# Graph attention where sets of twelve rows meet only the nodes they need, their rows gathered by indirect DMAs

## The chip, the core and the metric

The kernel runs on one core of one Trainium2 chip. The metric is the device time of one execution in microseconds; the kernel before takes 2598.82 us (median of 3 runs, 2598.19 to 2600.02). Engines are named as in the profile: PE is TensorE, DVE VectorE, ACT ScalarE, POOL GpSimd, SP the engine that only issues DMAs.

## The reference

Two layers of graph attention over 8 graphs of 2048 nodes that share one adjacency matrix `adj`, and a layer norm. The first layer has 4 heads of 64 features, the second one head.

```python
def _gat_layer(h, mask, b):
    scores = jnp.einsum('...nd,...md->...nm', h, h)
    scores = jnp.where(mask, scores, NEG)
    attn = jax.nn.softmax(scores, axis=-1)
    return jnp.einsum('...nm,...md->...nd', attn, h) + b
mask = graph + jnp.eye(N, dtype=graph.dtype) > 0
h = jnp.einsum('bnc,hdc->bhnd', x, Wh)
out_h = _gat_layer(h, mask[None, None], bh[None, :, None, :])
cat = jnp.transpose(out_h, (0, 2, 1, 3)).reshape(B, N, H * D)
z = jax.nn.leaky_relu(cat, negative_slope=0.2)
h2 = jnp.einsum('bnk,dk->bnd', z, Wo)
out2 = _gat_layer(h2, mask[None], bo)
z2 = jax.nn.leaky_relu(out2, negative_slope=0.2)
out = (z2 - mu) * jax.lax.rsqrt(var + LN_EPS) * gamma + beta
x = _layernorm(x + out, axis=-1)
```

The entry of `adj` for nodes n and m is 1 with a probability of 0.0039 times a weight of n and a weight of m, and the weights fall with the node's number: the first nodes have many neighbours (177, 130, 110 ...), those from number 56 on seven on average.

## The kernel before

Both kernels are two programs behind each other. `fast_kernel` shifts scores by a constant instead of each row's maximum, and writes a flag when its sums leave the range in which this is safe. `gat_kernel` reads the flag, and `general_kernel`, which is exact for all inputs, runs only if it is set. In the execution profiled it does not run.

The fast program has 20 units: four pairs of graphs, each with four units of the first layer (one graph, two heads) and one of the second (two graphs). A unit has 4 chunks of 512 nodes and for each of them 16 steps over the other nodes, 128 at a time: 1280 steps in all. The loop over `steps` writes out, step after step: `scores` (L560: 4 matmuls of 64x64 weights and 512 columns on the four quarters of the PE array, into a PSUM tile `s`; L563 on DVE takes the mask off; L564 on ACT is the exponential), and three steps later (`LAG`) `values` (L573: 4 matmuls with the exponentials as moving operand, added up in `o`). The sums of the exponentials are formed by `add_up` on POOL (L604) and by accumulating DMAs that POOL issues (L593), and joined by `sums` (L639). Every node meets every node; the mask adds a large negative number where `adj` has no entry.

What follows a chunk (`join`, `leaky`, `invert`, `scale`, `project`, `norm`) is handed to later steps by `at`, a table from step to jobs. `load_adj` (L478) brings `adj` in 32 pieces of 512 KB, `mask_rows` (L483) turns them into numbers on ACT, `mask_turn` transposes them. `prepare` turns a unit's maps with small matmuls of 64x64 weights and 64 columns (L438).

Order is fixed by the code: the fast program is written under a manual schedule, so each engine runs its instructions as written, and a semaphore holds one back only until its operands and its buffer are there.

## Time and profile before

| What | Value |
|---|---|
| median of 3 runs | 2598.82 us |
| the profiled execution | 2602.55 us |
| its span on the core | 2600.8 us |
| its granted PE clock | 0.991 |
| PE records of matmuls | 26414, two for each f32 matmul |
| PE, DVE, ACT, POOL busy | 97, 70, 66, 78% |
| DMA | 144027 packets, 289.62 MB, 111 GB/s on average |
| HBM read and written | 42.40 MB and 4.46 MB |

In a row of a group stand the line, the engine, the operation, output and inputs with their shapes, the count; after the bar the busy time in us and the mean time of one in ns; after the second bar the time that the engine idled before such instructions, and what ended the waits. Groups of weight loads are named PEld; they run beside the matmuls. Several matmuls run at once on parts of the array, so the mean time of one is longer than the distance between two starts.

### The profile page before, as it was taken

The page shows a single profiled execution, that of the slowest core. Times are in us where ns is not written, and L with a number is a line of the kernel's source. Part 1 is how long each engine was busy: PE and PEld are TensorE (multiplying, and loading weights), DVE is VectorE, ACT ScalarE, POOL GpSimd, SP SyncE. Part 2 cuts the span into 40 slices and gives each one's busy share as a digit, 9 for nine tenths or more (in the row PEclk, how much of TensorE's full clock was granted, in tenths as well). Part 3 has the DMA queues.
Part 4 walks back from the last instruction along what each step waited for, and adds up shares of the span by engine and source line. Part 5 has one row for each costly group of instructions (what it writes and reads, how often), then busy time and mean ns, then how long its engine had stood idle before and what let it go on. Part 6 is the DMA issues. An engine that isn't in the chain of part 4 may idle for free.

```text
span 2600.8 us, 61515 instructions
## 1 busy us (share of the span) xinstructions
PE 2512.0 (97%) x26414; PEld 891.4 (34%) x26414; DVE 1812.2 (70%) x1755; ACT 1706.5 (66%) x1721; POOL 2037.0 (78%) x1265
## 2 busy tenths in 40 slices
PE   7999999999999999999999899999999999999996
PEld 3333333333333333333333233333333333333332
DVE  5876677677777577666777676766676777676775
ACT  5776666666666566666666566666666666666664
POOL 5788788788767888778867887887888788875776
PEclk9999999999999999999999999999999999999998
DMA  4326566556555556656655465655565566655553
GB/s 138 104 77 120 102 116 128 102 107 122 114 100 115 114 107 113 132 101 113 118 116 109 96 121 112 128 110 103 113 116 107 107 123 118 116 112 98 115 113 79
DMA packets 144027, 289.62 MB, mean 111 GB/s; under 512 B 50658, under 2 KB 75298, under 8 KB 143746
## 3 DMA queue, kind: packets, MB, share of 16 engines
q0 software_dynamic: 65552, 238.32, 49.2%
q1 hardware_dynamic: 62722, 46.76, 6.1%
q8 instruction: 208, 3.41, 0.5%
q10 hardware_dynamic: 15472, 0.53, 0.5%
q14 instruction: 73, 0.60, 0.1%
HBM read 42.40 MB, written 4.46 MB: 18 GB/s over the span
## 4 chain that ended last, share of the span: by engine, by line
PE 72%; DMA 9%; POOL 5%; ACT 4%; DVE 4%; issue 3%; ACTq 1%; SPq 0%; POOLq 0%; DVEq 0%
PE s L560 34%; PE o L573 31%; PE pz L639 4%; DMA e<-e 3%; DVE e L563 3%; DMA zt<-zsb 3%; POOL acc L604 2%; DMA z<-rd 1%; ACT e L564 1%; DMA rd<-rt 1%; PE pn L438 1%; POOL acc L607 1%; ACTq L652 1%; PE o L682 1%; ACT hT L524 1%
## 5 line engine op out<-in xcount | busy, mean ns | idle before, releaser
L563 DVE TENSOR_TENSOR e<-s,mask 128x1024 f32<-128x1024 f32 x1280 | 1560.9, 1222 | 661.2 <-PE s L560 634.9
L564 ACT ACTIVATE e<-e,shifts 128x1024 f32<-128x1024 f32 x1280 | 1467.3, 1148 | 799.9 <-DVE e L563 753.1
L573 PE MATMUL o<-e,hN 64*64 64x512 f32 x10240 | 1332.8, 591 | 2.9 <-ACT h2T L689 2.1
L604 POOL TENSOR_TENSOR acc<-acc,e 128x1024 f32<-128x1024 f32 x452 | 1158.5, 2563 | 86.0 <-ACT e L564 71.4
L560 PE MATMUL s<-hT 64*64 64x512 f32 x8192 | 1076.0, 596 | 28.4 <-DVE e L563 9.4
L573 PEld LDWEIGHTS o<-e,hN 64*64 64x64 f32 x10240 | 391.9, 133 | 714.4 <-issue 586.8
L560 PEld LDWEIGHTS s<-hT 64*64 64x64 f32 x8192 | 296.2, 133 | 596.5 <-issue 436.7
L593 POOL DMA_DIRECT2D e<-e x454 | 398.5, 968 | 99.6 <-ACT e L564 61.6
L560 PE MATMUL s<-h2T 64*64 64x512 f32 x2048 | 267.8, 593 | 0.3 <-DVE e L563 0.2
L601 POOL TENSOR_TENSOR acc<-e,e 128x1024 f32<-128x1024 f32 x80 | 190.6, 2383 | 28.8 <-ACT e L564 18.8
L607 POOL TENSOR_TENSOR acc<-acc,e 128x1024 f32<-128x1024 f32 x60 | 142.1, 2368 | 76.6 <-DMA e<-e 75.6
L560 PEld LDWEIGHTS s<-h2T 64*64 64x64 f32 x2048 | 75.0, 134 | 137.5 <-issue 114.5
L639 PE MATMUL pz<-e,ones 128*32 128x512 f32 x616 | 116.4, 601 | 1.2 <-DVE e L563 0.7
L639 PE MATMUL pz<-acc,ones 128*32 128x512 f32 x320 | 85.4, 613 | 20.2 <-POOL acc L607 20.1
L734 POOL TENSOR_TENSOR st<-st,mhalf 128x8 f32<-128x8 f32 x32 | 57.3, 1791 | 49.7 <-ACT st L733 49.7
L673 POOL TENSOR_TENSOR z<-u,z 128x512 f32<-128x512 f32 x32 | 40.9, 1277 | 57.5 <-DMA z<-rd 48.8
L642 ACT COPY zsb<-pz 128x512 f32<-128x512 f32 x80 | 45.9, 574 | 52.3 <-PE pz L639 51.2
L673 POOL TENSOR_TENSOR u<-u,z 128x512 f32<-128x512 f32 x32 | 40.9, 1277 | 47.3 <-DMA z<-rd 40.5
L744 POOL TENSOR_TENSOR y<-y,st 128x512 f32<-128x512 f32 x15 | 15.6, 1041 | 74.1 <-ACT st L743 69.4
L627 DVE TENSOR_TENSOR u<-o,o 128x512 f32<-128x512 f32 x80 | 55.2, 690 | 6.9 <-ACT o L622 3.5
L618 DVE TENSOR_TENSOR o<-o,oj 128x512 f32<-128x512 f32 x80 | 55.9, 699 | 4.6 <-ACT oj L614 3.1
L552 DVE TENSOR_TENSOR hN<-pn,bhb 128x1024 f32<-128x1024 f32 x32 | 39.2, 1225 | 27.1 <-PE pn L438 26.9
(82 smaller groups left out, 769.4 us busy)
## 6 DMA issues: line engine op xcount, KB each, us to landing
e<-e POOLq DMA_DIRECT2D x454, 512.0 KB, 5.6
adj<-in_adj_dram SPq DMA_DIRECT2D x32, 512.0 KB, 4.6
z<-rd SPq DMA_DIRECT2D x128, 128.0 KB, 3.4
x<-in_x_dram SPq DMA_DIRECT2D x16, 256.0 KB, 4.1
xr<-in_x_dram SPq DMA_DIRECT2D x32, 128.0 KB, 2.4
out_dram<-y SPq DMA_DIRECT2D x32, 128.0 KB, 5.5
zt<-zsb SPq DMA_DIRECT2D x160, 2.0 KB, 5.0
zt<-zsb ACTq DMA_DIRECT2D x160, 2.0 KB, 5.4
```

What stands on the lines that cost most here:

```text
L560: nc.tensor.matmul(ps[k * 64:(k + 1) * 64, j, :], self.hT[rows, m * P + k * 64:m * P + (k + 1) * 64], self.hT[rows, c * W:(c + 1) * W], st ...
L563: nc.vector.tensor_tensor(e, ps, mask[c][:, m, :].unsqueeze(1).to_broadcast([P, 2, W]), OP.subtract)
L564: nc.scalar.activation(e, e, AF.Exp, bias=shifts[:, 1:2] if self.second else shifts[:, 0:1], scale=1.0)
L573: nc.tensor.matmul(self.O[c][j * D:(j + 1) * D, r, :], self.hN[rows, m, j * D:(j + 1) * D], e[rows, j, :], start=(m == 0), stop=(m == NB - 1))
L593: nc.gpsimd.dma_start(out=self.first[k], in_=e, accum_op=OP.add)
L601: nc.gpsimd.tensor_tensor(acc, self.acc, e, OP.add)
L604: nc.gpsimd.tensor_tensor(self.acc, self.acc, e, OP.add)
L607: nc.gpsimd.tensor_tensor(self.acc, self.acc, self.first[k], OP.add)
L618: nc.vector.tensor_tensor(b, b, self.t, OP.add)
L639: nc.tensor.matmul(pz[q:q + 32, :W], ones, terms[s * half + k][:, j, :], start=(k == 0), stop=(k == half - 1), tile_position=(0, q))
L673: nc.gpsimd.tensor_tensor(dst, self.u[c], self.z[c], OP.mult)
L734: nc.gpsimd.tensor_tensor(st[:, 2, :], st[:, 1, :], mhalf, OP.pow)
```

## The change

The fast program is replaced; the exact one stays. The flag's program and the check remain in kind, with other conditions.

The first 56 nodes (`HUB`) are treated as before in kind: each meets all nodes, in 16 blocks of 128 (`hub_scores`, `hub_values`), for all 8 graphs. The other 1992 nodes form 166 sets of 12 (`SET`): set s has the nodes 56 + s, 56 + s + 166, and so on. A set needs the union of its twelve rows of `adj`. The kernel makes one number per set and node: bit k is set where row k needs the node, times 2048, plus the node's number (`make_keys`: matmuls with powers of two add twelve rows of `adj` up). DVE picks for each set the 128 largest of these (`pick`: eight classes of 256 nodes by number modulo 8, the 32 largest of each by `max` and `match_replace`, eight at a time, then the 128 largest of those 256). A transpose makes them columns: `index` holds the node of each of the 128 slots, and `mask` which of the twelve rows need it. `over` keeps the last kept number of each class and set; if one is still a needed node, the flag is set. Sets are sorted in two rounds, 84 and 82 sets; the first in the hub phase, the second inside layer 1.

`table1` in DRAM has a row of 8 x 65 numbers for each node (8 graphs, 64 features and a one). An indirect DMA on POOL (`gather`) brings the 128 rows of a set, 266 KB. The column of ones makes each sum of exponentials a 65th column of the values. Scores of the first layer are x'(W'W)x: `gram` holds W'W for each head, `columns` multiplies it to the set's own twelve nodes, `scores` multiplies that to the gathered rows, turned by 64x64 matmuls with the identity (`turn`). The values are sums of x, and `heads` applies W after that. Two sets are a group; 83 groups run through layer 1 in a loop of stages written out by hand. `second_maps` and `second_rows` write the second layer's maps to `table2`, from which layer 2 gathers, four sets at a time (42 units); `back` and `norm_sets` bring its results to rows of 120 nodes for the two norms, in parts spread over units by `spread`.

The core of the diff (all of the function's lines of before are removed; PSUM has two buffers for each of the tags `s` and `o`; NG is 83, NU 42, LOOK 4):

```diff
-    epool = ctx.enter_context(tc.tile_pool(name="epool", bufs=13))
...
-    steps = [(u, c, m) for u in units for c in range(NC) for m in range(NB)]
-    total = len(steps)
...
+    rowp = ctx.enter_context(tc.tile_pool(name="rowp", bufs=12))
+    def two(name, tag="s"):
+        return psum.tile([P, 2, 512], F32, tag=tag, name=name)
+    def turn(tp, j, rows):
+        v = tp.rearrange("c r (j q i) -> c r j q i", j=2, q=Q)
+        for q in range(Q):
+            for p in range(2):
+                for r in range(2):
+                    nc.tensor.matmul(v[half(p), r, j, q, :], rows[half(r), 2 * q + p, :D], ident[half(r), half(r)],
+                                     start=True, stop=True)
...
+    def load_adj(r, c, t):
+        s0, n = ROUNDS[r]
+        raw = early.tile([84, 2, 512], I32, tag="raw", name=f"raw{r}_{c}_{t}", bufs=3)
+        nc.sync.dma_start(out=raw[:n], in_=byset[s0:s0 + n, 2 * t:2 * t + 2, c * 512:(c + 1) * 512])
+        a = early.tile([84, 2, 512], BF16, tag="a", name=f"a{r}_{c}_{t}", bufs=7)
+        nc.gpsimd.tensor_scalar(a[:n], raw[:n], 1.0, 0.0, OP.min, OP.max)
...
+    def top(src, dst, last):
+        def job():
+            nc.vector.max(out=dst, in_=src)
+            if not last:
+                nc.vector.match_replace(out=src, in_to_replace=dst, in_values=src, imm_value=-1.0)
+        return job
...
+    def gather(table, s, layer):
+        t = rows[layer, s] = rows_tile(f"g{layer}_{s}")
+        nc.gpsimd.indirect_dma_start(out=t.rearrange("p b k -> p (b k)"), out_offset=None, in_=table,
+                                     in_offset=bass.IndirectOffsetOnAxis(ap=index[:, s:s + 1], axis=0))
...
+    def values(g):
+        op = two(f"o{g}", "o")
+        e = es[g % 2]
+        for j in range(2):
+            rw = rows.pop((1, 2 * g + j))
+            for q in range(Q):
+                for p in range(2):
+                    c0 = (p * 8 + q * 2 + j) * M
+                    nc.tensor.matmul(op[half(p), j, q * K1:(q + 1) * K1], e[:, c0:c0 + 64], rw[:, 2 * q + p, :],
+                                     start=True, stop=True)
+        osb = held["o", g] = work.tile([P, 2, Q, D], F32, tag="osb", name=f"osb{g}")
+        invert(op, rall[:, g, :].rearrange("p (s q) -> p s q", s=2), osb, P, Q)
...
+    for i in range(-2, NG + 5):
+        for g in ([i + LOOK] if i > -2 else range(0, LOOK - 1)):
+            if 0 <= g < NG:
+                for j in range(2):
+                    gather(table1, 2 * g + j, 1)
...
+        if 0 <= i < NG:
+            values(i)
+        if 0 <= i + 1 < NG:
+            scores(i + 1)
+        if 0 <= i + 2 < NG:
+            tp, t = turn_group(1, i + 2, "s")
+            nc.scalar.copy(t, tp)
+        if 0 <= i - 1 < NG:
+            heads(i - 1)
+        if 0 <= i < NG:
+            turn_values(i)
+        if i >= 0:
+            for _ in range(2):
+                if pieces:
+                    r, c, k = pieces.pop(0)
+                    load_adj(r, c, k)
+                    if k == SET // 2 - 1:
+                        make_keys(r, c)
...
+    for u in range(-2, NU + 10):
+        for v in ([u + 3] if u > -2 else range(1, 2)):
+            if 1 <= v < NU:
+                for s in sets[v]:
+                    gather(table2, s, 2)
...
+        if 0 <= u + 1 < NU:
+            scores2(two(f"s2_{u + 1}", "o"), sets[u + 1], es[(u + 1) % 2])
+        if 0 <= u + 2 < NU:
+            for g in sorted({s // 2 for s in sets[u + 2]}):
+                tp, t = turn_group(2, g, "s")
+                (nc.scalar.copy if g % 2 else nc.vector.tensor_copy)(t, tp)
+        if 0 <= u < NU:
+            values2(sets[u], es[u % 2])
```

How the order changes on the engines is shown at three places; a row has the line, the operation, output and inputs by name and number, the shape and how often it comes in a row. First PE in the middle of layer 1. Before, scores `s` and values `o` alternate:

```order
L560 MATMUL s_2_11_3178<-hT_0_184 64x512 x4
L573 MATMUL o_2_3038<-e_2_8_3130,hN_2004 64x512 x4
L560 MATMUL s_2_12_3191<-hT_0_184 64x512 x4
L573 MATMUL o_2_3038<-e_2_9_3143,hN_2004 64x512 x4
L560 MATMUL s_2_13_3204<-hT_0_184 64x512 x4
```

Now one turn of the loop has these rows (`hyr` holds the second layer's maps, the set's own columns and the second layer's rows; `o` the values, `s` the scores, `t` the turned rows `g`, `cat` the heads, `ot` the turned values):

```order
L792 MATMUL hyr_7629<-z_7452,woT 64x96 x4
L737 MATMUL hyr_7629<-xT,gram 64x96 x8
L798 MATMUL hyr_7629<-ident,own 48x128 x2
L767 MATMUL o_7651<-g_76_7029,e_152 64x65 x8
L767 MATMUL o_7651<-g_77_7031,e_152 64x65 x8
L749 MATMUL s_7671<-y_7494,xTg_39_7590 64x48 x32
L509 MATMUL t_40_7706<-ident,g_80_7327 64x64 x16
L509 MATMUL t_40_7706<-ident,g_81_7329 64x64 x16
L525 MATMUL cat_7741<-otb_7623,whT 64x96 x8
L779 MATMUL ot_7755<-ident,osb_7668 64x48 x16
```

Eight matmuls of 512 columns a step have become 118 of 48 to 128 columns a group; the whole fast program has 18062 matmuls for 13721. Second, DVE and ACT at the same place. DVE's turn of the loop, from the copy of the own columns `y` to the half of `leaky` that writes `z`:

```order
L739 COPY y_7643<-hyr_7629 128x384
L803 COPY rowt_156<-hyr_7629 48x2x64
L515 RECIPROCAL rall<-o_7651 128x8
L516 TENSOR_TENSOR osb_7668<-o_7651,rall 128x512
L752 TENSOR_TENSOR e_153<-s_7671,mask 128x768
L534 SCALAR_TENSOR_TENSOR z_7750<-cat_7741,bhp,z_7750 128x192 x2
```

ACT's turn beside it:

```order
L756 ACTIVATE e_152<-e_152,shifts 128x768
L865 COPY xTg_41_7888<-t_41_7855 128x1024
L533 ACTIVATE z_7899<-cat_7890,bhf 128x192 x2
L781 COPY otb_7921<-ot_7904 128x384
L794 COPY own<-hyr_7927 128x96
L803 COPY rowt_154<-hyr_7927 48x2x64
```

Where a step before had one pass of 1024 on each, a group has six passes on each, and `leaky` stands behind the mask on DVE and behind the copy of the turned rows on ACT. Third, POOL in layer 2. Before, POOL adds exponentials and issues accumulating DMAs:

```order
L593 DMA e_0_0_7837<-e_0_8_7986 128x1024
L593 DMA e_0_1_7853<-e_0_9_8000 128x1024
L604 TENSOR_TENSOR acc_0_7926<-acc_0_7926,e_0_10_8015 128x1024
L604 TENSOR_TENSOR acc_0_7926<-acc_0_7926,e_0_11_8031 128x1024
L734 TENSOR_TENSOR st_3_8057<-st_3_8057,mhalf 128x8
```

Now it has a unit's four gathers into `g`, and now and then a power for a norm:

```order
L721 DMA g_44_16762<-table_136,index 128x520
L721 DMA g_45_16764<-table_136,index 128x520
L721 DMA g_46_16766<-table_136,index 128x520
L721 DMA g_47_16768<-table_136,index 128x520
L973 TENSOR_TENSOR st_15988<-st_15988,mhalf 120x8
L973 TENSOR_TENSOR st_16383<-st_16383,mhalf 120x8
```

The sums on POOL and the accumulating DMAs are gone; 332 gathers have come, each held back in POOL's order until one of the 12 row buffers `g` is free.

More of the change, by code (lines that the diff above doesn't have):

```diff
@@ L39 @@
 FMAX = 3.4028234663852886e38
-BIG = 255.0
+HUB = 56
+SET = 12
 SHIFT1 = 78.0
@@ L459, in fast_kernel @@
[L459 to L468 removed]
+    table1 = dram.tile([N, ROW], F32, name="table1")
@@ new lines, in turn_values @@
+    def turn_values(g):
+        pt = two(f"ot{g}", "o")
+        osb = held.pop(("o", g))
+        for q in range(Q):
+            for j in range(2):
+                for p in range(2):
+                    r = slice(p * 64, p * 64 + M)
+                    nc.tensor.matmul(pt[half(j), p, q * M:(q + 1) * M], osb[r, j, q, :], ident[r, r], start=True, stop=True)
+        ot = held["ot", g] = work.tile([P, H, 2 * Q * SET], F32, tag="ot", name=f"otb{g}")
+        nc.scalar.copy(ot.rearrange("c h (p n) -> c h p n", p=2),
+                       pt[:, :, :Q * M].rearrange("c p (n h) -> c h p n", h=H))
@@ new lines, in hub_block, with hub_turn @@
+    def hub_block(w):
+        for j in range(2):
+            t = rows["h", 2 * w + j] = rows_tile(f"gh{2 * w + j}")
+            i = 2 * w + j
+            nc.sync.dma_start(out=t.rearrange("p b k -> p (b k)"), in_=table2[i * P:(i + 1) * P, :])
+    def hub_turn(w):
+        tp = two(f"th{w}")
+        for j in range(2):
+            turn(tp, j, rows["h", 2 * w + j])
+        t = held["T", "h", w] = work.tile([P, 2, 512], F32, tag="xTg", name=f"xTgh{w}", bufs=3)
+        nc.scalar.copy(t, tp)
@@ new lines, in fast_kernel @@
+    nc.vector.tensor_reduce(tot[:, 4:5], over.rearrange("p r k -> p (r k)"), AX.X, OP.max)
+    nc.vector.tensor_scalar(tot[:, 4:5], tot[:, 4:5], float(N), None, OP.is_lt)
+    nc.vector.tensor_reduce(tot[:, 5:6], tot[:, 0:5], AX.X, OP.min)
+    pf = two("pf")
+    nc.tensor.matmul(pf[0:1, 0, 0:1], tot[:, 5:6], ones, start=True, stop=True)
+    fl = late.tile([1, 1], I32, name="fl", bufs=1)
+    nc.vector.tensor_scalar(fl, pf[0:1, 0, 0:1], P - 0.5, None, OP.is_lt)
+    nc.sync.dma_start(out=flag, in_=fl)
```

932 lines of the change are left out of this document (536 added, 396 removed).

## The prediction

> **What bounds the kernel now.** I read the page from the top (span and busy shares), then the chain that ended last, then the two dearest groups.
>
> ```profile
> span 2600.8 us, 61515 instructions
> ...
> PE 2512.0 (97%) x26414; PEld 891.4 (34%) x26414; DVE 1812.2 (70%) x1755; ACT 1706.5 (66%) x1721; POOL 2037.0 (78%) x1265
> ...
> PE 72%; DMA 9%; POOL 5%; ACT 4%; DVE 4%; issue 3%; ACTq 1%; SPq 0%; POOLq 0%; DVEq 0%
> ...
> L573 PE MATMUL o<-e,hN 64*64 64x512 f32 x10240 | 1332.8, 591 | 2.9 <-ACT h2T L689 2.1 <-ACT e L564 0.7
> ```
>
> TensorE is busy 97% and idles 2.9 us before 10240 value records: it is the bound, and every score is computed, masked or not. The change takes most scores away, so what counts is what a small matmul costs. The timeline of TensorE has one burst of them between two of the large ones (start, length, group):
>
> ```profile
> 906.12 1.11 PE L438 MATMUL pn<-ident,hT 64*64 64x64 f32 x64
> 907.05 1.04 PE L560 MATMUL s<-hT 64*64 64x512 f32 x8
> 907.92 1.04 PE L573 MATMUL o<-e,hN 64*64 64x512 f32 x8
> ```
>
> Each f32 matmul leaves two records. Starts differ by 0.93 us for 64 records of 64 columns: **14.5 ns each**. Eight of 512 columns take 0.87 us, four quarters of the array running at once: 0.85 ns a column on one quarter, 0.21 on four, 0.42 on two.
>
> **Layer 1, one pair of sets (83 of them).** Records on TensorE, in the order of the change's listing of one turn of the loop: 8 of 96 columns on half the array (0.32 us), 16 such (0.64), 4 of 128 (0.21), 32 of 65 for the values (0.87), 64 of 48 for the scores (at 14.5 ns 0.93), 64 turns (0.93), 16 of 96 on a quarter (0.32), 32 of 48 (0.46). Sum 4.7 us. The other engines' durations:
>
> ```profile
> L563 DVE TENSOR_TENSOR e<-s,mask 128x1024 f32<-128x1024 f32 x1280 | 1560.9, 1222 | 661.2 <-PE s L560 634.9 <-POOL acc L604 10.7 <-issue 5.7
> L564 ACT ACTIVATE e<-e,shifts 128x1024 f32<-128x1024 f32 x1280 | 1467.3, 1148 | 799.9 <-DVE e L563 753.1 <-issue 37.2 <-ACT e L564 0.9
> ...
> L618 DVE TENSOR_TENSOR o<-o,oj 128x512 f32<-128x512 f32 x80 | 55.9, 699 | 4.6 <-ACT oj L614 3.1
> ...
> L614 ACT COPY oj<-o 128x512 f32<-128x512 f32 x80 | 45.6, 570 | 1.3 <-PE o L573 1.0
> ...
> L524 ACT COPY hT<-ph 128x1024 f32<-128x1024 f32 x32 | 31.8, 995 | 1.3 <-PE ph L522 1.2
> ...
> L660 DVE RECIPROCAL rt<-zall 128x8 f32<-128x8 f32 x80 | 16.3, 203 | 2.8
> ...
> L731 DVE TENSOR_REDUCE st<-sq 128x8 f32<-128x512 f32 x16 | 11.0, 686 | 11.8 <-ACT sq L718 11.8
> ...
> L507 DVE COPY whT<-pw 128x256 f32<-128x256 f32 x1 | 0.4, 425 | 7.7 <-PE pw L506 7.7
> ```
>
> Read between these rows by width, VectorE does 384 + 64 + reciprocal + 512 + 768 + 2x192 in 3.4 us, ScalarE 768 + 1024 + 2x192 + 384 + 96 + 64 in 3.6. No engine is full, so the period comes from a loop. The accumulator `o` has two buffers for three uses, and the values of pair i+1 take the buffer that the heads of pair i-1 leave when `leaky` has read it. Going round: values 0.87, reciprocal and product 0.20 + 0.70, mask 0.96 (queued behind them on VectorE), exp 0.87, copy of the turned rows 1.0 and two `leaky` passes 0.66 (in ScalarE's order behind the exp), VectorE's last half 0.35, seven hand-overs 0.4. **6.0 us a pair.** The hand-overs are an estimate from these rows of the timeline, where the exp begins 0.04 us after the mask ends; those to and from TensorE are taken a little longer:
>
> ```profile
> 900.36 1.22 DVE L563 TENSOR_TENSOR e<-s,mask 128x1024 f32<-128x1024 f32 x1 [0.49 <-PE s L560]
> ...
> 901.62 1.15 ACT L564 ACTIVATE e<-e,shifts 128x1024 f32<-128x1024 f32 x1 [0.57 <-DVE e L563]
> ```
>
> Pairs fall into three stretches. 57 run free: 342 us. In 14 the second sort shares VectorE: four jobs a pair, a max and a replace over 256 elements each, priced with the 256-wide row (0.425 each, so 3.4 us); with the two copies that stand behind them (0.56 + 0.28) the loop becomes 9.15 us, 128 us in all. In the first 12 pairs the second half of adj arrives.
>
> **Second-half adj: the number of engines.** 24 transfers of 82 rows x 2 x 2 KB = 336 KB, three in flight, with the pass over each on POOL ahead of later gathers and the keys in TensorE's queue: if they are late, all is late.
>
> ```profile
> q1 hardware_dynamic: 62722, 46.76, 6.1%
> ...
> adj<-in_adj_dram SPq DMA_DIRECT2D x32, 512.0 KB, 4.6
> z<-rd SPq DMA_DIRECT2D x128, 128.0 KB, 3.4
> x<-in_x_dram SPq DMA_DIRECT2D x16, 256.0 KB, 4.1
> xr<-in_x_dram SPq DMA_DIRECT2D x32, 128.0 KB, 2.4
> out_dram<-y SPq DMA_DIRECT2D x32, 128.0 KB, 5.5
> zt<-zsb SPq DMA_DIRECT2D x160, 2.0 KB, 5.0
> ...
> rd<-rt SPq DMA_DIRECT2D x64, 4.0 KB, 2.9
> ...
> flag<-fl SPq DMA_DIRECT2D x1, 0.0 KB
> ```
>
> The window of 14 to 20 us, with DMA share and GB/s last:
>
> ```profile
> 14.00:20.00 6.00, 5.18 (x56) 1.91 (x57) 1.94 (x2) 3.04 (x4) 1.62 (x4) 1.00 0.99 320
> ```
>
> A transfer's data packets are the contiguous runs of its tile. By the shapes in the code SP's 465 transfers hold 55296 of them beside the flag (adj 32x512, z 128x64, x 16x128, xr and out 32x128 each, zt 128x64 + 32x128, rd 64x128). 62722 (the first figure of the queue's row) less those is 7426 = 464x16 + 2: a transfer of 64 or 128 rows ends in 16 packets, one per DMA engine, and the one-row flag in one, beside its data. So the rows decide how many engines serve a transfer, and 82 = 2x41 rows go in equal shares to two engines and not to 16. The window (DMA share 0.99, 320 GB/s) gives 20.2 GB/s an engine. Ends: on 16 engines a transfer takes 1.0 us and is hidden; on two 8.3 us, 200 us for 24. I take **200 us**, since equal shares fit what the packets show. [...]
>
> **Gathers.** 332 on POOL, 266 KB each, an operation that the trace does not have.
>
> ```profile
> L604 POOL TENSOR_TENSOR acc<-acc,e 128x1024 f32<-128x1024 f32 x452 | 1158.5, 2563 | 86.0 <-ACT e L564 71.4
> L593 POOL DMA_DIRECT2D e<-e x454 | 398.5, 968 | 99.6 <-ACT e L564 61.6 <-DMA e<-e 34.7 <-issue 3.1
> ...
> L734 POOL TENSOR_TENSOR st<-st,mhalf 128x8 f32<-128x8 f32 x32 | 57.3, 1791 | 49.7 <-ACT st L733 49.7
> ...
> L468 POOL DMA_DIRECT2D bob<-in_L_gnn_bo_dram x2 | 1.1, 569 | 0.0
> ```
>
> From 0.57 (128 plain rows) to 2.56 (POOL's dearest pass); I take 0.97, the other transfer that POOL issues row by row. Landing: 4.1 us, as x, of equal size. In layer 1 that is 1.9 us of 6.0, issued four pairs ahead: hidden. **In layer 2 it is not.** Its 12 row buffers are three units of four sets; the gathers of unit u+3 wait, in POOL's queue, until `values2` of unit u has read its rows, and TensorE wants them in the next unit. From the end of `values2`: the first buffer was free 0.7 us earlier, the fourth gather starts 2.9 us after that (2.2), lands at 6.3, 64 turns to 7.2, `values2` (64 records) to 8.2. **8.2 us a unit, 42 units, 344 us.** Beside it TensorE has 256 records, 4.7 us or less; VectorE 384 + a 1024 copy 1.2 + the norms (14 passes of 0.69 and small ones, 10.5 us per 2.5 units) and waits, 6.7; POOL 3.9 + pow 1.4.
>
> **The rest.** The adj passes are ScalarE's now:
>
> ```profile
> L483 ACT ACTIVATE mrow<-adj,shifts 128x1024 bf16<-128x1024 int32 x32 | 36.3, 1134 | 0.0
> ```
>
> On POOL one may take 1.13 to 2.56 us; I take 2.0, nearer to the row of its own engine. Start and blocks 0 to 3: 24 such passes and 8 us before them, 56. Blocks 4 to 8, under the first sort: 87 steps of 0.425, masks 7, their own VectorE 12: 56. Seven blocks more: TensorE 3.7 (turns, 32 records of 224 columns, 32 of 65 on the whole array), with waits 4.6: 32. Hub ends: twice eleven dependent steps of 0.5, and 6 for the first groups: 17. Between the layers: five draining turns at 2, 7 for `table2` to land and be read, eight steps of layer 2's hubs at 3.3 (a 1024 copy, an 896 exp, the masks, hand-overs), 6 to fill: 49. The end: a norm's 10.5 on VectorE, `back` out and in at 2.9 each (as `rd`), its steps' hand-overs and powers 6, `out` 5.5, the flag 2: 30. These are estimates from the rows shown.
>
> Sum: 56 + 56 + 32 + 17 + 200 + 128 + 342 + 49 + 344 + 30 = 1254, and 1.75 outside the span (profiled 2602.55 against 2600.8): 1256. The median shown, 2598.82, is 0.14% under the profiled execution: **1254**.
>
> **Rivals.**
> 1. All 16 engines serve the 82-row transfers. Nothing in the trace has such a row number. Twelve pairs then cost 6.5 us with the keys' matmuls, 78 for 200: **1132**.
> 2. A gather costs POOL 2.5 us, for it must read 128 indices. Layer 1 still hides 5.0; in layer 2 the fourth starts at 6.8, 12.8 us a unit, +194: **1448**. Against it: 0.57 and 0.97 for the plain ones.
> [...]
> 4. Slower: a set needs over 128 slots or a class over 32, or a sum leaves its bounds; the flag is set and the exact program runs behind. Its values alone are 5120 matmuls of 256 columns on the whole array, two records each: 2.2 ms, so over **3450**. Counted on the reference's inputs, the fullest set needs 119 slots, the fullest class 26, and logs of the sums lie from -57.7 to 78.7 where -63 to 83 pass.
>
> **How the numbers follow.** Forecast 48%, rivals 24, 17, 8 and 3%. The range runs from rival 1 with the loop or the gather somewhat cheaper (0.57 a gather takes 50 us off) to rival 2 with 20 more: 1040 to 1470. 0.2% is about what a measurement can tell from no change; only rival 4 is not faster by more.
>
> **What would show it.** Second-half adj landing in 20 us or more, and TensorE waiting for POOL's `a` and the keys in the first 12 pairs (16 engines: under 6 us). Pairs 6.0 us apart, with `o` waiting for `leaky`. Units 8 us apart, with the turns of layer 2 waiting for DMA; if for POOL's queue and 12 us, the gather's price is wrong. Units under 7 us would mean that rows land sooner than 4 us. TensorE's records of 64 columns at 14 ns, or not.

## The result, and the profile after

The changed kernel takes **1776.5 us** (median of 4 runs, 1767.7 to 1788.1) beside 2599.4 us for the kernel before (4 runs, 2598.2 to 2601.9): ratio 0.684, 95% interval 0.680 to 0.688. The profiled execution took 1767.7 us, 512 us more than the 1255.8 us of the prediction's sum. The sign was right, the size was not. One remark is needed for later numbers: the experiments ran on four chips, and the unedited changed kernel takes 1771 to 1789 us on one of them and 1956 us on another, so each experiment is read against the run of the changed kernel that has the same time for a pair of sets.

The page of the changed kernel: span, busy shares, the granted clock in 40 slices, the chain of work that ended last, and four of its groups and issues (columns as before).

```profile
span 1765.9 us, 77071 instructions
...
PE 1205.0 (68%) x35983; PEld 1063.5 (60%) x35983; DVE 705.3 (40%) x1427; ACT 453.4 (26%) x818; POOL 449.3 (25%) x467
...
PEclk9669866666777887887877888887866665666665
...
PE 9%; issue 8%; DMA 6%; POOL 4%; DVE 3%; ACT 1%; SPq 1%; POOLq 0%; DVEq 0%; ACTq 0%
...
L721 POOL DMA_INDIRECT g<-table,index x332 | 323.3, 974 | 1040.3 <-PE o L767 595.2
L509 PE MATMUL t<-ident,g 64*64 64x64 f32 x10624 | 278.0, 268 | 62.5 <-DMA g<-table,index 50.1
...
L644 POOL TENSOR_SCALAR a<-raw 84x1024 bf16<-84x1024 int32 (+1 forms) x48 | 49.7, 1036 | 211.2 <-DMA raw<-in_adj_dram 211.0
...
g<-table,index POOLq DMA_INDIRECT x332, 4.2
```

No engine is full any more. TensorE went from 97% to 68%, with 9600 more records than before, and its clock, nearly full in the kernel before (0.991), is now between 0.6 and 0.9 of full in almost every slice (0.736 on average). A gather costs GpSimd 0.974 us and lands after 4.2 us, as priced (0.97, 4.1).

Three stretches of layer 1 and the units of layer 2 in windows (length; busy time and count for PE, PEld, DVE, ACT, POOL; granted clock, DMA share, GB/s):

```profile
200.00:400.00 200.00, 95.59 (x2585) 76.09 (x2577) 40.49 (x77) 36.47 (x73) 50.61 (x60) 0.69 0.23 71
400.00:575.00 175.00, 115.86 (x3268) 104.86 (x3272) 90.25 (x237) 43.89 (x92) 28.49 (x31) 0.74 0.20 54
575.00:1150.00 575.00, 411.02 (x12143) 366.97 (x12136) 182.36 (x361) 173.96 (x364) 96.33 (x102) 0.80 0.21 55
...
1300.00:1690.00 390.00, 306.03 (x11530) 281.98 (x11534) 203.37 (x334) 94.83 (x136) 189.48 (x170) 0.64 0.50 137
```

These counts give the pace: a pair has 236 records of matmuls, so the third row is 12143 / 236 = 51.5 pairs, 11.2 us each; a unit has 320, so the fourth is 36.0 units, 10.8 us each. The prediction had 6.0 and 8.2. By its terms:

| Stretch | predicted us | measured us |
|---|---|---|
| start to the first pair (56 + 56 + 32 + 17) | 161 | 192 |
| 12 pairs while the second half of adj arrives | 200 | 208 |
| 14 pairs with the second sort | 128 | 174 |
| 57 free pairs | 342 | 626 |
| between the layers | 49 | 72 |
| 42 units | 344 | 426 |
| end, from the last values | 30 | 68 |

One free pair in the timeline of the changed kernel (start, length, engine, group, and in brackets the idle time before it with what ended it):

```profile
800.10 0.25 ACT L794 COPY own<-hyr 128x96 f32<-128x96 f32 x1
...
800.41 1.52 PE L737 MATMUL hyr<-xT,gram 128*64 128x96 f32 x16 [1.85 <-ACT own L794]
802.04 0.56 DVE L739 COPY y<-hyr 128x384 f32<-128x384 f32 x1 [1.75 <-PE hyr L737]
...
802.66 0.67 PE L798 MATMUL hyr<-ident,own 128*48 128x128 f32 x4 [0.73 <-DVE y L739]
...
803.11 1.95 PE L767 MATMUL o<-g,e 128*64 128x65 f32 x32
...
804.99 2.08 PE L749 MATMUL s<-y,xTg 64*64 64x48 f32 x64
...
806.82 1.89 PE L509 MATMUL t<-ident,g 64*64 64x64 f32 x64
...
808.51 0.52 PE L525 MATMUL cat<-otb,whT 64*64 64x96 f32 x16
...
811.78 0.54 PE L737 MATMUL hyr<-xT,gram 128*64 128x96 f32 x4 [1.46 <-ACT own L794]
```

Two things are to be seen. TensorE waits twice in a turn, 1.85 and 0.73 us, and for nothing that it needs: the score maps, the columns and the rows of one turn stand in one PSUM tile, `hyr`, in different places, and a write to that tile is put behind an earlier read by another engine (the copy to `own`, the copy to `y`). And its records are slow: 64 turns from 806.82 to the next group at 808.51 are 26 ns each, for 14.5 predicted. The granted clock of this stretch (last but two in the row) says why:

```profile
803.10:809.70 6.60, 6.39 (x212) 6.28 (x209) 2.15 (x4) 1.80 (x3) 1.89 (x2) 0.59 0.35 91
```

14.5 ns at a clock of 0.59 would be 25. In the trace the clock is one half from 801.64 to 808.46 and full behind that, so the 0.80 of the free pairs is an average of the two. Over the run the waits come to this (waits view; total, times, longest):

```profile
PE hyr L737 <- ACT own L794: 157.1, 78, 2.6
PE hyr L798 <- DVE y L739: 75.4, 77, 2.7
...
PE t L509 <- DMA g<-table,index: 50.1, 53, 3.0
```

### The profile page after: what moved, and what is told of

Its sections match the earlier page's. It is cut to its first block, busy times and chain, and to the rows that moved or that the text cites. A ratio compares the mean times of both kernels' runs of the same rounds, so it can differ in the third digit from the quotient of the medians.

```text
span 1765.9 us, 77071 instructions
## 1 busy us (share of the span) xinstructions
PE 1205.0 (68%) x35983; PEld 1063.5 (60%) x35983; DVE 705.3 (40%) x1427; ACT 453.4 (26%) x818; POOL 449.3 (25%) x467
## 5 line engine op out<-in xcount | busy, mean ns | idle before, releaser
L721 POOL DMA_INDIRECT g<-table,index x332 | 323.3, 974 | 1040.3 <-PE o L767 595.2
L509 PE MATMUL t<-ident,g 64*64 64x64 f32 x10624 | 278.0, 268 | 62.5 <-DMA g<-table,index 50.1
L509 PEld LDWEIGHTS t<-ident,g 64*64 64x64 f32 x10624 | 252.3, 178 | 76.4 <-DMA g<-table,index 33.7
L737 PE MATMUL hyr<-xT,gram 128*64 128x96 f32 x1296 | 125.6, 348 | 157.9 <-ACT own L794 157.1
L767 PEld LDWEIGHTS o<-g,e 128*64 128x64 f32 x2656 | 149.8, 212 | 0.5 <-ACT otb L781 0.2
L767 PE MATMUL o<-g,e 128*64 128x65 f32 x2656 | 147.4, 296 | 0.0
L749 PE MATMUL s<-y,xTg 64*64 64x48 f32 x5312 | 144.4, 258 | 1.1 <-issue 0.5
L898 PE MATMUL s<-own,xTg 64*64 64x12 f32 x5312 | 119.7, 224 | 27.1 <-issue 26.3
L749 PEld LDWEIGHTS s<-y,xTg 64*64 64x64 f32 x5312 | 127.3, 171 | 15.6 <-issue 1.5
L898 PEld LDWEIGHTS s<-own,xTg 64*64 64x64 f32 x5312 | 112.9, 167 | 35.5 <-issue 30.9
L798 PE MATMUL hyr<-ident,own 128*48 128x128 f32 x332 | 52.8, 417 | 81.2 <-DVE y L739 75.4
L644 POOL TENSOR_SCALAR a<-raw 84x1024 bf16<-84x1024 int32 (+1 forms) x48 | 49.7, 1036 | 211.2 <-DMA raw<-in_adj_dram 211.0
L739 DVE COPY y<-hyr 128x384 f32<-128x384 f32 x81 | 44.9, 554 | 121.2 <-PE hyr L737 121.1
L1123 DVE COPY xTg<-t 128x1024 f32<-128x1024 f32 x42 | 51.4, 1224 | 75.4 <-PE t L509 75.4
```

Of the source, the lines that this page charges most:

```text
L509: nc.tensor.matmul(v[half(p), r, j, q, :], rows[half(r), 2 * q + p, :D], ident[half(r), half(r)], start=True, stop=True)
L721: nc.gpsimd.indirect_dma_start(out=t.rearrange("p b k -> p (b k)"), out_offset=None, in_=table, in_offset=bass.IndirectOffsetOnAxis(ap=ind ...
L737: nc.tensor.matmul(py[half(p), h * 96:(h + 1) * 96], gram[:, h, half(p)], src, start=True, stop=True)
L749: nc.tensor.matmul(sp[half(r), p, (q * 2 + j) * M:(q * 2 + j + 1) * M], xt[half(p), r, j, q, :], y[half(p), (j * Q + q) * M:(j * Q + q + 1 ...
L767: nc.tensor.matmul(op[half(p), j, q * K1:(q + 1) * K1], e[:, c0:c0 + 64], rw[:, 2 * q + p, :], start=True, stop=True)
L798: nc.tensor.matmul(pr[j * 64:j * 64 + 48, :], own[:, g, j * 48:(j + 1) * 48], ident, start=True, stop=True)
```

## Experiments

**e1: two tiles for the shared one.**

```diff
-        hyr = two(f"hyr{i}") if i > -3 else None
-        ... second_maps(i - 3, hyr[:, 0, :]); columns(i + 2, hyr[:, 1, :]); second_rows(i - 4, hyr[:, 0, 128:256])
+        hm, hy = two(f"hm{i}"), two(f"hy{i}")
+        ... second_maps(i - 3, hm[:, 0, :]); second_rows(i - 4, hy[:, 0, 128:256]); columns(i + 2, hy[:, 1, :])
```

> Only layer 1's ring is changed: the score maps and the pair (scores turned, columns) get a PSUM tile each instead of one for all three, and TensorE does maps, rows, columns in that order. Theory A (the tile that three stages share makes TensorE wait for ScalarE's copy of the columns and then for VectorE's leaky step in every turn, 1.46 to 1.85 and 0.7 us of an 11.1 us turn, and the waits let the granted clock fall, which stretches the 9.0 us of matmuls): both waits go from the list, a free pair takes 6.5 to 8 us, the whole 1500 to 1600 us. Theory B (the small matmuls simply cost 25 to 29 ns each at the clock this chip grants them): only the waits go, 2 to 2.5 us a pair over 83 pairs, the whole 1570 to 1640 us, with the 64 records of a group still at 1.8 us. Theory C (the loop through ScalarE and VectorE bounds it, and TensorE's waits are only where it shows): no change over 2%.

Measured 1707.5 us. The waits view of this run shows why it is less than theory A had: the columns stand behind the copies of the rows now, in the tile that those two still share.

```profile
PE hy L737 <- DVE rowt L803: 165.4, 77, 5.4
```

One wait went and the other came back in another place; 69 us under the median of the changed kernel. It decides nothing between A and B.

**e2: a tile of its own for each half of the leaky step.**

```diff
-        z = work.tile([P, HP, 2, n], F32, tag="z", name=f"z{name}")
+        z = [work.tile([P, 2, n], F32, tag=f"z{hp}", name=f"z{name}_{hp}") for hp in range(HP)]
```

> Only the leaky step's z is changed: one tile per pair of heads instead of one for both, in both layers. In one tile, ScalarE's second half waits for VectorE's first (0.48 us in a turn of layer 1, 40.2 us in sum over the run). If the loop TensorE columns, values, scores, turn, copy, leaky, own sets layer 1's pace (theory C), a pair gets about 0.45 us shorter, the whole 83 x 0.45 = 37 us shorter, near 1735 us. If TensorE's matmuls at a low clock set it (theory B), the whole stays within 15 us of 1766 to 1788.

Measured 1772.1 us, no change, but the edit missed its aim. ScalarE's second half still waits for VectorE's first, as often and as long as in the changed kernel (40.2 us, 83 times):

```profile
ACT z L533 <- DVE z L534: 40.3, 83, 0.5
```

So it was not the output `z` that ordered them; what is left in common is the PSUM tile `cat` that both read, which no run tested. The price of that order was not measured.

**e3: rounds of 96 and 70 sets.**

```diff
-    ROUNDS = ((0, 84), (84, NS - 84))
+    ROUNDS = ((0, 96), (96, NS - 96))
```

> Only the split of the sets' 166 block rows into two rounds is changed, 96 + 70 for 84 + 82, so that both counts divide by 16 or 14. Theory of the prediction (a transfer whose rows do not divide by 16 is cut on two engines, 8.3 us for each 82-row transfer): the twelve pairs that load the second half fall from 208 us to between 100 (the matmul pace of the pairs around) and 135 us, the whole by 70 to 105 us, to 1670 to 1705 us. Rival (those pairs are bound by the matmuls or by GpSimd's reduction of the loaded rows): no change over 2%.

Measured 1702.9 us, 65 to 85 under the changed kernel, where 70 to 105 was expected. The window that had 2585 records in 200 us:

```profile
200.00:400.00 200.00, 146.41 (x4039) 126.04 (x4037) 79.36 (x178) 56.46 (x113) 62.47 (x75) 0.79 0.33 84
```

Half as much work again passes in the time in which the loads arrive, and GpSimd's waits for them fall from 211.0 to 125.0 us. Loads of 96 or 70 rows came sooner here than loads of 82. The changed kernel alone says the same of 84 rows: its first 24 passes over the loaded rows, of 84 rows each, start 2.1 us apart (from 15.0 to 64.2 us), the 24 of 82 rows 8.8 us apart (from 194.7 to 396.0). Its trace shows the engines, too: an 82-row load ends in 2 packets of 4 bytes, and between 186.5 and 193.5 us, when little but such loads moves, the DMA share is 0.14, 2.2 of the 16 engines. So the two-engine step was right for 82 rows. For every number that 16 does not divide, as the expectation has it, it is not: an 84-row load ends in 14 such packets.

**e4: four times the columns at the same number of matmuls.** In `scores2`, each matmul moves 48 columns; the 36 too many are overwritten by the next.

```diff
-                        nc.tensor.matmul(sp[half(r), p, c0:c0 + SET], ..., own[..., a0:a0 + SET], ...)
+                        nc.tensor.matmul(sp[half(r), p, c0:c0 + 48], ..., flat[half(p), a0:a0 + 48], ...)
```

> Only layer 2's own scores are changed: each matmul moves 48 columns instead of 12, the 36 more being overwritten by the matmuls behind it, so that TensorE does the same count of records with four times the columns. Theory 1 (the granted clock follows how much of the time the array moves columns): the clock of the 42 units rises from 0.67 to 0.85 or more and a unit falls from 10.15 to about 8.5 us, the whole by 50 to 70 us. Theory 2 (the clock falls because of the waits between the matmuls, 1 us in a unit, whatever they move): clock 0.62 to 0.72, and a unit as long as now or up to 1.5 us longer, the whole 1766 to 1850 us.

Measured 1769.9 us. The window of the units in this run:

```profile
1300.00:1690.00 390.00, 267.86 (x11690) 239.08 (x11688) 203.41 (x334) 96.19 (x137) 192.34 (x173) 0.84 0.51 137
```

The clock went from 0.64 to 0.84 (theory 1, just short of the 0.85 named), and the unit stayed: 11690 records are 36.5 units, 10.7 us. TensorE got faster and waited longer. With these gathers the clock was not what set a unit.

**e5, e7: 16 row buffers in layer 2, alone and with e4.**

```diff
+    rowp2 = ctx.enter_context(tc.tile_pool(name="rowp2", bufs=16))
```

> Only layer 2's gathers are changed: they land in 16 buffers of their own instead of the 12 of layer 1. GpSimd waits about 4.7 us in each unit for TensorE to free a buffer, and TensorE about 1 us for the gather that starts so late. If the chain value matmuls, gather issues, landing, turn is what sets a unit (10.15 us), four buffers more let it fall to the matmuls' own 9 us or below: 42 to 80 us off the whole, 1690 to 1735 us. If the matmuls at their low clock set it, the unit stays within 0.3 us and the whole within 15 us of 1766 to 1788.

> e4 and e5 together: 48 moving columns for 12 in layer 2's own scores (which raised the granted clock of the units from 0.63 to 0.86 and left a unit at 10 us), and 16 row buffers. If, as e4 says, the clock is not what sets a unit, but the gathers that wait for a buffer, this falls as far as e5 or further: a unit 7 to 8.5 us, the whole 1640 to 1710 us. If neither sets it, the whole stays above 1740 us.

Measured 1954.9 and 1955.3 us: far slower, and already in layer 1, which the edit does not touch. That asked for a control.

**c0: nothing edited.**

> The kernel as changed, nothing edited, as a control beside the runs of this call. In e5, layer 1's program is the same as in the kernel as changed, and yet its pairs took 12.4 us for 11.1, with pauses of 0.4 to 1.1 us inside the scores' matmuls that TensorE entered for no wait the profile shows. If these pauses belong to e5's edit, this run repeats 1768 to 1788 us without them. If they belong to the chip or core that the runs of that call were given, they can show here too, with about 100 us more in layer 1.

Measured 1955.8 us, against 2599.2 for the kernel before beside it. So the 16 buffers cost nothing; the changed kernel itself is 10% slower there. Layer 1 in 300 us, first of the run of the result, then of this control:

```profile
600.00:900.00 300.00, 215.80 (x6372) 192.97 (x6372) 95.26 (x189) 89.50 (x187) 51.00 (x54) 0.80 0.21 55
```

```profile
600.00:900.00 300.00, 211.77 (x5734) 186.43 (x5729) 88.91 (x177) 80.51 (x169) 44.68 (x48) 0.77 0.19 49
```

6372 / 236 is 27.0 pairs, 11.1 us; 5734 is 24.3 pairs, 12.3 us. The runs e1 to e4, c1, f4 and f5 are from a chip of the first kind, the others from three of the second. Beside c0, e5 and e7 show no gain: on that kind of chip neither the buffers nor, with them, the clock moved the units.

**e6, e6b: write all three, then read.**

```diff
+        for g, put, drain, at in ((i - 4, second_rows, rows_out, hyr[:, 0, 128:256]),
+                                (i - 3, second_maps, maps_out, hyr[:, 0, :]),
+                                (i + 2, columns, columns_out, hyr[:, 1, :])) if i > -3 else ():
+            if 0 <= g < NG:
+                put(g, at)
+                jobs.append((drain, g, at))
+        for drain, g, at in jobs:
+            drain(g, at)
```

> Only the order in layer 1's ring is changed: the rows, the score maps and the columns keep their one tile, but all three are written first and read afterwards, so that no write of TensorE stands behind a read of that tile in the same turn (in the kernel as changed it did twice, and with two tiles in e1 still once: columns behind the copies of the rows, 1.8 us). Theory A: both waits go, TensorE stays busy through the turn, its clock stays up, a free pair falls from 11.1 us to 6 to 7.5, the whole to between 1440 and 1560 us. Theory B (the matmuls cost 25 to 29 ns each whatever stands around them): a pair 8.6 to 9.2 us, the whole 1590 to 1640 us. Theory C (another loop, over ScalarE and VectorE, is the limit): a pair at or above 10 us, the whole over 1680 us.

> e6 again, beside the control. In e6 both waits were gone and the granted clock was 0.92, the 64 records of a group ran in 0.93 us when they ran on, and a pair still took 9.2 us, because the scores' matmuls paused three times, 0.6 us each. If the pauses come with the chip, this run has none where the control has none, and a pair takes 6.5 to 7.5 us (the whole 1500 to 1580 us). If they come with TensorE running at full clock, they are here as in e6, and the whole is 1680 to 1710 us.

Measured 1698.7 and 1696.1 us, the second beside c0's 1955.8: **260 us** less. Both waits on `hyr` are gone and the clock is up; the timeline of e6 shows what is left:

```profile
806.37 1.11 PE L769 MATMUL o<-g,e 128*64 128x65 f32 x32
807.41 0.81 PE L751 MATMUL s<-y,xTg 64*64 64x48 f32 x35
808.63 0.33 PE L751 MATMUL s<-y,xTg 64*64 64x48 f32 x4 [0.41 <-issue]
809.38 0.34 PE L751 MATMUL s<-y,xTg 64*64 64x48 f32 x5 [0.43 <-issue]
810.11 0.51 PE L751 MATMUL s<-y,xTg 64*64 64x48 f32 x18 [0.39 <-issue]
...
810.48 1.08 PE L509 MATMUL t<-ident,g 64*64 64x64 f32 x60
811.36 0.24 PE L525 MATMUL cat<-otb,whT 64*64 64x96 f32 x1
```

60 turns run from 810.48 to 811.36, 14.7 ns each, at a granted clock of 1.00: the burst's price of the prediction. But TensorE stops three times inside the scores, for nothing that the profile shows ("issue"), in this turn and in most others (90 times in the 33 turns of e6b's 300 us). The 300 us of e6b:

```profile
600.00:900.00 300.00, 240.69 (x7685) 214.58 (x7687) 113.36 (x231) 110.02 (x228) 62.50 (x66) 0.93 0.26 68
```

32.6 pairs, 9.2 us. Theory B's 9 us came out, but not by its mechanism: the records were cheap where they ran on, and 1.4 us of the 9.2 are stops for which no cause is shown (44.9 us in these 300).

**e8, e9: no gathers, and plain transfers in their place.** The edits stand in `gather`, for layer 1:

```diff
+        if layer == 1 and s >= 12:          # e8
+            rows[layer, s] = first[s % 12]
+            return
+        if layer == 1:                      # e9
+            nc.sync.dma_start(out=t.rearrange("p b k -> p (b k)"), in_=table[s * 11:s * 11 + P, :])
+            return
```

> e6 with layer 1's gathers left out from the thirteenth set on: the pairs go on with the twelve row buffers that were gathered first, so that GpSimd and the row transfers are idle while the pairs run. So that the sums stay finite, the scores of sets and of layer 2 are multiplied by 0 before the exponential, in the same instruction. Theory E (the pauses come with the gathers: they begin 0.7 or 0.95 us after GpSimd starts the first gather of a turn): no pause, a pair 6.5 to 7.2 us. Theory D (TensorE's own stream of 472 instructions a turn comes no faster): pauses and a pair as in e6b, within 0.5 us.

> e6 with layer 1's gathers replaced by plain transfers of the same size (128 rows of 520 numbers, rows in a block, issued by SyncE), so that GpSimd issues nothing while the pairs run, and the row transfers stay. The choice of rows is left out, and the scores of sets and of layer 2 are multiplied by 0 before the exponential, in the same instruction. If e6's pauses come from the transfers' traffic, they are here too and a pair takes 9 us or more; if they come from GpSimd's issue of indirect transfers, a pair takes 7.0 to 7.4 us, as without gathers (e8: 7.04).

The whole is 7.9 ms in both, which fits a set flag and the exact program run behind it, and says nothing; layer 1 is read alone. The 300 us of e8, then of e9:

```profile
600.00:900.00 300.00, 258.44 (x9995) 237.99 (x9991) 143.46 (x296) 144.77 (x295) 0.00 (x0) 1.00 0.05 12
```

```profile
600.00:900.00 300.00, 255.39 (x9826) 235.37 (x9819) 141.12 (x292) 144.68 (x293) 0.00 (x0) 1.00 0.32 86
```

42.4 and 41.6 pairs: **7.1 and 7.2 us**, at full clock, although e9 moves more bytes per microsecond (86 GB/s) than e6b (68). So the 2 us do not come with the amount of traffic. The stops inside the scores are gone in both, but stops of the same kind stand before other matmuls (32.6 us in e8 and 37.6 in e9, 0.8 and 0.9 us a pair); the larger part of the 2 us is that the matmuls of a pair keep TensorE busy for 6.1 us (258.44 us for 42.4 pairs) where they took 7.4 in e6b. e9 changes the issuer, the kind of transfer and the choice of rows together, and both runs multiply the scores by 0, so which of these counts is not shown. What TensorE then needs for itself is in e8's timeline:

```profile
701.74 0.42 PE L808 MATMUL hyr<-ident,own 128*48 128x128 f32 x4
701.99 0.50 PE L800 MATMUL hyr<-z,woT 128*64 128x96 f32 x8
702.32 1.50 PE L743 MATMUL hyr<-xT,gram 128*64 128x96 f32 x16
703.74 1.15 PE L775 MATMUL o<-g,e 128*64 128x65 f32 x32
704.82 1.15 PE L757 MATMUL s<-y,xTg 64*64 64x48 f32 x64
705.79 0.43 PE L509 MATMUL t<-ident,g 64*64 64x64 f32 x16
```

Start to start: rows 0.25, maps 0.33, **columns 1.42**, values 1.08, scores 0.97. The columns were priced at 0.64. In e8 TensorE is the limit: 6.1 us busy, 0.8 in stops and 0.2 in waits are the 7.1.

**e10: half as many matmuls for the scores.**

```diff
-                for p in range(2):
-                    for r in range(2):
-                        nc.tensor.matmul(sp[half(r), p, ...], xt[half(p), r, j, q, :], ...)
+                for p in range(2):
+                    nc.tensor.matmul(sp[:, p, ...], xt[half(p), j, q, :], ...)
```

> e6 with half as many matmuls for the scores of the sets and of layer 2: 64 x 128 stationary blocks for 64 x 64, the same columns moved, two at a time for four, so that the array is busy as long; a turn issues 204 matmuls for 236, a unit of layer 2 256 for 320. Theory D (supply of instructions): a pair falls by 32 x 2 x 18 ns = 1.15 us, a unit by 64 x 2 x 16 ns = 2.0 us, the whole by 150 to 190 us. Theory E (gathers): the pauses stay, a pair falls by less than 0.4 us, and the whole by less than 50 us.

Measured 1705.1 us beside e6b's 1696.1: a pair fell by 0.5 us (9.2 to 8.7, by counts of records; 1.15 was expected), the units not at all, and the whole did not gain. The stops fell from 1.4 to 0.6 us a pair (19.3 us in 300, all before `t`). So fewer matmuls shorten the stops, as theory D (the supply of instructions) says, and leaving the gathers out shortens them too, as theory E (the gathers) says; neither accounts for all.

**f2: e2 to e6 together.**

> e2, e3, e4, e5 and e6 together, to see whether the parts add. With e3's 65 us off, theory A of e6 gives 1640 - 65 to 1440 - 65 less what 16 buffers bring: 1320 to 1480 us. If the parts get in each other's way, it stays within 30 us of the best of them alone.

Measured 1633.0 us: e6's gain and e3's 65, and nothing from the parts in layer 2.

**e11: gathers a unit earlier, and the norms' loads by ScalarE.**

```diff
-        for v in ([u + 3] if u > -2 else range(1, 2)):
+        for v in ([u + 4] if u > -2 else range(1, 3)):
...
-            nc.sync.dma_start(out=t..., in_=back[a:b]...)
+            nc.scalar.dma_start(out=t..., in_=back[a:b]...)
```

> The kernel as changed, with two edits in layer 2: the gathers of a unit are issued one unit earlier and land in 20 buffers for 12 (every two of five units in eight buffers of their own), and the loads of the norms are issued by ScalarE instead of SyncE. Layer 1 is as it was, and tells by its pairs (11.2 or 12.4 us) whether this chip shows the pauses. Gather theory (values free a buffer, four gathers are issued in 5 us, the last lands 4.2 us later, is turned, and only then come the next values): a unit falls from 10.2 (11.8 with the pauses) to 9.0 (10.5) or below, the whole by 50 to 100 us. Rival (TensorE's own work at the clock it is granted, or GpSimd's pauses, bound it): a unit stays within 0.3 us. The end after the last unit falls from 66 to about 50 us, since loads no longer stand behind the stores of the norm before.

Measured 1949.7 us, pairs of 12.5: a chip like c0's. The unit stays at 12.7 us (c0: 12.4, both by counts of records). TensorE's longest waits in 420 us of units, in c0 and then here:

```profile
PE s L898 <- issue: 84.7, 209, 1.7
```

```profile
PE t L509 <- issue: 46.9, 77, 2.9
PE s L905 <- issue: 46.6, 86, 1.8
```

These rows do not say whether TensorE waits for rows: the profiles of c0 and e11 (and of f3, f4 and f5) tell no gather's landing, and such a wait, too, would stand under "issue" in them. In the changed kernel's run, which has landings for half of them, the same line had (in the 390 us of the window above):

```profile
PE t L509 <- DMA g<-table,index: 48.0, 50, 3.0
```

What is measured is the pace: earlier gathers brought nothing where there are pauses, and for the other kind of chip this run decides nothing. The end did get shorter; the wait of TensorE's last matmul for the norms, in c0 and then here:

```profile
PE pf L1142 <- DVE tot L1140: 56.8, 1, 56.8
```

```profile
PE pf L1149 <- DVE tot L1147: 47.8, 1, 47.8
```

**f3: e2, e3, e6 and e11.**

> e2, e3, e6 and e11 together. f2 had 1633 us in a call whose chip showed the pauses; with the gathers a unit earlier and the shorter end, 1560 to 1610 us there, or 1400 to 1480 us on a chip without pauses. If layer 2 is bound by something else, 1620 us or more with pauses.

Measured 1627.4 us (4 runs, 1622.7 to 1637.5; ratio to before 0.628, 0.625 to 0.630), again with the pauses. What it has over f2 is little beyond the shorter end.

**c1, f4, f5: both limits of layer 2 lifted, on a chip without the pauses.** f4 is f3 with e4's columns, f5 is f4 with e10's blocks.

> The kernel as changed once more, timed beside f4 and f5 on the same chip: 1768 to 1788 us where GpSimd's gathers do not make TensorE pause (pairs 11.2 us, units 10.2 us), 1940 to 1970 us where they do (pairs 12.4 us, units 11.8 us).

> f3 with e4's 48 moving columns for 12 in layer 2's own scores. In e4 the clock rose and the gathers held the unit; in e11 and f3 the gathers came in time and TensorE, at a granted clock of 0.62 to 0.64, held it. Where both are lifted a unit should fall from 11.9 to 10.5 us or less with the pauses (41 x 1.4 = 57 us off f3's 1627, so 1560 to 1590 us), or from 10.2 to 8 to 9 us without them (1400 to 1450 us). If only the pauses hold the unit, it stays at 11.5 us or more and the whole at 1610 us or more.

> f4 with e10's 64 x 128 stationary blocks for the scores of the sets and of layer 2, so half as many of these matmuls for the same columns. In e10 a pair fell by 0.45 us beside e6b (8.75 for 9.2) and a unit by nothing, when the gathers still held the unit. Theory D for layer 2 (the pauses are a supply of instructions that runs out): a unit falls by another 0.8 to 1.2 us below f4's, the whole by 60 us or more. Otherwise the whole is within 40 us of f4's.

Measured: c1 1779.5 us (1770.8 to 1788.9); f4 **1424.9** (1421.0 to 1432.6), ratio to before 0.549 (0.546 to 0.551); f5 **1402.2** (1386.6 to 1408.6), ratio 0.538 (0.534 to 0.541). Both beat the kernel before and the changed one. The windows of f4, layer 1 and layer 2:

```profile
520.00:820.00 300.00, 262.24 (x8991) 229.76 (x8988) 131.60 (x267) 127.59 (x267) 71.79 (x76) 1.00 0.30 78
```

```profile
1000.00:1320.00 320.00, 215.81 (x10072) 196.43 (x10071) 175.73 (x291) 82.75 (x118) 169.86 (x150) 0.86 0.54 145
```

And the units of c1, on the same chip:

```profile
1300.00:1690.00 390.00, 300.32 (x11403) 274.55 (x11399) 202.47 (x331) 93.75 (x133) 189.51 (x169) 0.65 0.50 136
```

Pairs 38.1 in 300 us, **7.9 us** for 11.1 at full clock. Units 31.5 in 320 us, 10.2 us for c1's 10.9: not the 8 to 9 expected. f5 is 23 us under f4, inside the 40 us of "otherwise", but its units fell as theory D had it. A unit has 256 records there:

```profile
1000.00:1320.00 320.00, 287.71 (x8896) 271.29 (x8894) 192.29 (x319) 91.13 (x130) 185.54 (x162) 0.87 0.58 157
```

34.8 units, **9.2 us** for f4's 10.2. In f4's 320 us TensorE stands 104 us with no cause shown (44.0 before `t`, 40.4 before `s`, 19.2 before `o`), in f5's 32. So the score matmuls hold part of f4's unit; whether some of its 104 us are waits for rows, its trace cannot tell. Nor was f3 run on a chip without pauses, so how much of the 0.7 us from c1 to f4 the gathers alone would have brought is open.

## Why the prediction was right and wrong

**The loop of layer 1, "6.0 us a pair", is the step that failed**: 284 of the 512 us, and the same loop runs under most of the 46 of the sort's pairs. (How the 9.15 us of those comes from 6.0, 3.4 and 0.84 the prediction does not say, all three together are 10.2; measured were 12.4.) Three errors lie in it.

1. The list of what follows what in a turn took the writes to `hyr` as free. It followed the buffers of `o` and never asked what the columns and rows wait for in a tile that three stages share. These waits took 1.85 and 0.73 us of the turn shown, and TensorE, the work of which was to lie hidden at 4.7 us, became a link of the loop.
2. With such waits the clock is not full: 0.80 in the free pairs, 0.59 in the stretch shown, and records there 26 ns apart. Undoing the order of writes and reads (e6b) brought the clock to 0.93 and 260 us back beside c0 (0.77); f4's pairs run at 1.00. The prediction had the burst's 14.5 ns throughout, and at full clock that is right (14.7 in e6). The clock fell with no gap over 2.6 us in the free pairs.
3. TensorE's own share was too small: 6.1 us busy at full clock (e8), more than the loop's 6.0, for a sum of 4.7. The largest part is the columns, 1.42 us for 0.64; the values took 1.08 for 0.87. The score maps, of the same shape, came at their price (0.33 for 0.32), so the half-array price was not wrong in itself: at full clock in the changed kernel's trace the columns' records, too, start two and two, 7 ns apart, but one pair of records each 0.167 us, where the maps have 0.083. What differs in the code is the operand that moves: the columns read `xT` in steps of 166 numbers, the maps read `z` in order. No run tested this. With no gathers and no wait on `hyr` the pair is 7.1 us, the least that was seen.

**Second-half adj, 200 us: right** (208), mechanism and size. The row number decided: passes 8.8 us apart at 82 rows and 2.1 at 84, loads that end in 2 packets and in 14, and GpSimd's waits for loads down from 211.0 to 125.0 us with 96 and 70 rows (e3); rival 1 falls. Of POOL's pass the price was double (1.04 us for 2.0), and hidden.

**The gather's price, 0.97 us and 4.1 us to land: right** (0.974 and 4.2), both taken from other transfers by likeness; rival 2 falls. So does rival 4: no run of the changed kernel went to the exact program.

**Layer 2, "8.2 us a unit": 10.1 on average, 10.8 in the steady stretch**, 82 us in all. The chain of gather, landing and turn was there (TensorE waited 50.1 us for `g`), but its links were priced for a full clock, and TensorE's own work, predicted as 4.7 us or less beside the 1.0 of `values2`, is 306 of 390 us in the window, 8.5 us a unit at a clock of 0.64. The clock alone changed nothing (e4), nor did buffers or earlier gathers on chips with pauses (e5, e7, e11); clock and gathers together gave 0.7 us a unit (f4), and half as many matmuls for the scores another 1.0 (f5).

**Sort steps 0.425: right** (421 and 405 ns in the groups of the changed kernel). The 31 us before the first pair and the 23 between the layers were estimates from rows, and no run took them apart.

**The end, 30 us: 68.** One norm was counted; three were left, one behind the other on VectorE, and their loads stood in SyncE's queue behind the stores of the norm before. Moving the loads (e11) took 9 us off; the rest, by the timeline, is the three norms themselves.

## What to carry to other kernels

Where an engine is to be hidden, list for each of its instructions what it waits for, tile by tile: the stages that share the PSUM tile `hyr` here waited for each other though each has its own bytes (157.1 and 75.4 us in the run), and writing all of them before reading any ended that at no further instruction (e6). Price small matmuls at the clock of a TensorE that waits (turns were 26 ns apart at 0.59, 14.7 at 1.00), and count records against the window, not busy time: a stage whose clock rises and whose pace stays (e4: 0.64 to 0.84, 10.8 and 10.7 us a unit) is held by another thing as well, so lift that one too before dropping the first.

## What was not expected of the hardware

- The granted clock rose with the columns moved, at the same number of matmuls: 48 columns for 12 in 128 of a unit's 320 records raised it from 0.64 to 0.84, though TensorE's waits for rows in the 390 us went from 48.0 to 58.0 us (e4).
- On three of the four chips TensorE stopped for 0.4 us and more, up to three times in a turn, while GpSimd issued indirect transfers (e6, e6b); with plain transfers of the same size a pair lost 2 us less, and shorter stops stood elsewhere (e9); with fewer matmuls the stops were shorter, too (e10, f5). In the unedited kernel a pair is 12.3 us there for 11.1, the whole 1956 for 1777 us (c0). On the fourth chip such pauses are short. The scores' group in 300 us of layer 1, in e6b and then in f4, with what stood before it:

```profile
L751 PE MATMUL s<-y,xTg 64*64 64x48 f32 x2112 | 68.3, 229 | 41.8 <-issue 40.9
```

```profile
L755 PE MATMUL s<-y,xTg 64*64 64x48 f32 x2432 | 71.3, 224 | 7.8 <-issue 7.3
```

  That is 1.3 us a pair in the one and 0.2 in the other. Why the chips differ is open.
